# Two-layer graph network on one core: the first two basis products of the first layer as 15 block products of thirds

## The chip, the core and the metric

The kernel runs on one core of a Trainium2 chip. TensorE (PE) multiplies and writes its results to PSUM, which has eight banks; VectorE (DVE) and ScalarE (ACT) read PSUM and do elementwise work; GpSimd (POOL) and SyncE (SP) issue most DMAs here. Each engine has its own queue and works through it in order; semaphores hold an instruction until what it needs is there. The metric is the device time in microseconds. All values are fp32.

## The reference, cut to what matters

A block of graph attention over 384 nodes comes first, then a relational graph convolution of two layers (the node feature width is 768, with six relations and four bases):

```python
def _rgcn_conv(x, src, dst, edge_type, basis, comp, root, bias):
    W = jnp.einsum('rb,bio->rio', comp, basis)
    h_all = jnp.einsum('ni,rio->rno', x, W)
    ...
    agg = jax.ops.segment_sum(msg, dst, num_segments=n)
    return agg + x @ root + bias
...
x = jax.nn.relu(h_text @ w_in + b_in)
for l in range(L):
    h_in = x
    x = _rgcn_conv(x, src, dst, edge_type, basis[l], comp[l], root[l], conv_bias[l])
    x = jax.nn.relu(x)
    x = x + h_in
    x = _batchnorm(x, bn_gamma[l], bn_beta[l])
```

The kernel computes the sum in another order: for each basis b it forms H_b = x · basis[l, b], a product of a 384x768 by a 768x768 matrix, and then multiplies the four H_b by four 384x384 matrices At_b, which are the normalised counts of edges A_r weighted with comp (the "mixes").

## The kernel before, in words

**Stages.** Layer norm and attention take the first part of the run. The projection `w_in` then leaves its result transposed in `XT`: 128 partitions, six chunks of 128 features, 384 nodes. Each of the two layers then has four bases, the product with `root`, the product with At and the batch norm. PE, DVE, ACT, POOL and SP run in program order (`manual_schedule`), so the order of the Python code is the order in each queue.

**One base.** For a base the weights lie in three tiles `w[0]` to `w[2]`, each 128 partitions by 2 by 768. Of the three blocks of 128 nodes, the third (n = 2) is multiplied directly (banks `pe` and `pf`, 12 products of 384 columns). Nodes 0 and 1 go by a product of 2x2 blocks that needs seven block multiplications in place of eight: `pa`, `pb`, `pc`, with the node sums `S` (from `node_sums`, L915, once a layer) and the weight sums `T` and `T4` (from `weight_sums`, L923, and `last_sums`, L932, for each base; nine VectorE operations). That is 21 products of 384 columns, so 33 in a base. `rest()`, the last block of a base, is issued inside the next base. The results go to `H_` by copies on ACT and additions on DVE (L991 to L1002).

**Banks.** `next_bank` takes the PSUM bank that was used longest ago among those allowed; `ring` holds the order.

**Loads.** `wload` puts a tile of 768 KB into one of five buffers (`wpool`), as four DMAs on SP. `w_first`, five of these tiles, is issued during attention; `load_basis` issues the rest.

**Work put between.** `go_between(l, b, c)` issues, at fixed places in bases 2 and 3 of the first layer, what prepares At: `share(r)` (L358: a matmul with ones, two ACT operations, a reciprocal and a multiplication on DVE) and `mix` (L341: At from A; 20 of these operations of VectorE follow the last addition of base 3). The counts A come from tables in memory, gathered by POOL's DMAs at L850 to L854 after its last scatter.

**Room.** `S`, `T4` and `H_` live in a pool `cp` that is opened when the attention pool closes; `T` takes the buffers tagged `hT` and `mask8`. In the stage after the bases, `spaces` (L1025 to L1035) reuses such room for the feature sums.

Of the kernel before, what the change touches and what calls it, by code (L numbers as in the profile page):

```python
# [10 lines left out]
F32 = mybir.dt.float32  # L11
# [3 lines left out]
AF = mybir.ActivationFunctionType  # L15
# [12 lines left out]
KC = DC // P  # L28
HC = DC // 2
HN = N // 2  # L30
R = 6
# [12 lines left out]


BQ, BK, BV, BIQ, BIK, BIV, B_IN, CB, GAM, BET, NCOL = 0, 8, 16, 24, 32, 40, 48, 54, 66, 78, 90

# [4 lines left out]
def gnn_kernel(ctx: ExitStack, tc: tile.TileContext, out, x, edges, chunks, cols, rows, small,  # L52
               wq, wk, wv, wiq, wik, wiv, wo, w_in, basis, root, w_out):
    nc = tc.nc
# [298 lines left out]
    def add_up(r):  # L353
        sums[r] = late.tile([P, N], F32, tag="sum", name="sum", bufs=4)
        nc.gpsimd.tensor_tensor(sums[r], A[:, r, 0, :], A[:, r, 1, :], ALU.add)
        nc.gpsimd.tensor_tensor(sums[r], sums[r], A[:, r, 2, :], ALU.add)

    def share(r):  # L358

        ps = next_bank("ps_cnt", [i for i in range(8) if i not in taken])  # L360
        nc.tensor.matmul(ps[:, :N], ones, sums[r], start=True, stop=True)
        rn = late.tile([P, N], F32, tag="rn", name="rn", bufs=2)

        nc.scalar.activation(rn, ps[:, :N], AF.Relu, bias=minus)
        nc.scalar.activation(rn, rn, AF.Identity, bias=ones[:, 0:1])
        nc.vector.reciprocal(rn, rn)
        nc.vector.tensor_tensor(A[:, r], A[:, r], rn[:, None, :].to_broadcast([P, NT, N]), ALU.mult)
        if r + 4 < R:
            add_up(r + 4)


    with ExitStack() as inner:
# [262 lines left out]
        At = late.tile([P, B, NT, N], F32, name="At")  # L635
        A = late.tile([P, R, NT, N], F32, tag="A", name="A")

        prA = keep.tile([P, KD, N], F32, tag="hT", name="prA")
# [92 lines left out]
        for g in range(STEPS + 1):  # L731
            f = g + LEAD
            if g < STEPS:
                turn_probs(g)
            if f < STEPS:
                exponents(f)
            if f - 1 in total:
                normalise(f - 1)
            if f + 1 < STEPS:
                scores(f + 1)  # L740
            if g == STEPS:
                ps_y = next_bank("ps_y", (0,))
                multiply_o(ps_y, 2, 0, range(KD - 1))
            if g > 0:
                gather(g - 1)
            if f + 2 == STEPS:

                w_x = [act_tile("w_x") for _ in range(2)]
                for half in range(2):
                    load_rows(w_x[half], w_in[half])  # L750
                w_first = [wload(basis[0, 0, part], (2, DC), "w_c") for part in range(3)]
                w_first += [wload(basis[0, 1, part], (2, DC), "w_c") for part in range(2)]
        soft_stack.close()
# [152 lines left out]
    with tc.tile_pool(name="conv", bufs=1) as cp:  # L906
# [4 lines left out]
        def block(X, n, i):  # L911

            return X.rearrange("p (c i) n -> p i c n", i=2)[:, i, :, n * P:(n + 1) * P]

        def node_sums(X):  # L915
            S = cp.tile([P, 4, 3, P], F32, tag="S", name="S")
            for i, a, b, op in ((0, block(X, 1, 0), block(X, 1, 1), ALU.add), (1, S[:, 0], block(X, 0, 0), ALU.subtract),
                                (2, block(X, 0, 0), block(X, 1, 0), ALU.subtract),
                                (3, block(X, 0, 1), S[:, 1], ALU.subtract)):
                nc.vector.tensor_tensor(S[:, i], a, b, op)  # L920
            return S

        def weight_sums(w):  # L923
            T13 = keep.tile([P, 3, 2, HC], F32, tag="hT", name="T13")
            T2 = keep.tile([P, 3, HC], F32, tag="mask8", name="T2")
            for c in range(3):
                nc.vector.tensor_tensor(T13[:, c], w[c][:, :, HC:], w[c][:, 0, :].rearrange("p (o d) -> p o d", o=2),
                                        ALU.subtract)
                nc.vector.tensor_tensor(T2[:, c], w[c][:, 1, HC:], T13[:, c, 0], ALU.subtract)
            return T13[:, :, 0], T2, T13[:, :, 1]  # L930

        def last_sums(w, T2):  # L932
            T4 = cp.tile([P, 3, HC], F32, tag="T4", name="T4")
            for c in range(3):
                nc.vector.tensor_tensor(T4[:, c], w[c][:, 1, :HC], T2[:, c], ALU.subtract)
            return T4

        w_first = [w_first[:3], w_first[3:]]

        def load_basis(l, b):  # L940
            w = w_first.pop(0) if w_first else []
            return w + [wload(basis[l, b, part], (2, DC), "w_c") for part in range(len(w), 3)]

# [17 lines left out]

        S = node_sums(XT)
        w = load_basis(0, 0)
        T = weight_sums(w)
        for l in range(L):

            H_ = cp.tile([P, B, NT, DC], F32, tag="H", name="H")
            rest = lambda: None
            for b in range(B):
                hs = [[H_[:, b, n, i * HC:(i + 1) * HC] for i in range(2)] for n in range(NT)]  # L970
# [21 lines left out]
                nc.vector.tensor_tensor(hs[0][0], hs[0][0], pb, ALU.add)  # L992
                times(pc, S[:, 0], lambda c: T[0][:, c], True)
                nc.scalar.copy(hs[2][0], pe)
                nc.scalar.copy(hs[2][1], pf)
                nc.scalar.copy(hs[1][1], pc)
                times(pa, S[:, 1], lambda c: T[1][:, c])
                nc.scalar.copy(hs[0][1], pa)
                times(pc, S[:, 3], lambda c: w[c][:, 1, HC:])
                nc.vector.tensor_tensor(hs[0][1], hs[0][1], pc, ALU.add)  # L1000
                times(pa, S[:, 2], lambda c: T[2][:, c])
                nc.vector.tensor_tensor(hs[1][1], hs[1][1], pa, ALU.add)  # L1002
# [14 lines left out]
            for k in range(KC):  # L1017
# [5 lines left out]
                go_between(l, B, k)  # L1023
            room2 = keep.tile([P, KD * N], F32, tag="hT", name="room2")
            spaces = [room2[:, 2304:]]  # L1025
            if l + 1 < L:
                spaces += [v.rearrange("p i k o -> p (i k o)")[:, i * 768:(i + 1) * 768] for v, n in
                           ((cp.tile([P, 4, 3, P], F32, tag="S", name="sums"), 2),
                            (wpool.tile([P, 2, 6, P], F32, tag="w", name="sums"), 2)) for i in range(n)]
                spaces.append(cp.tile([P, 3, HC], F32, tag="T4", name="sums").rearrange("p c d -> p (c d)")[:, :768])  # L1030
                w = load_basis(l + 1, 0)
# [48 lines left out]
            T1, T2 = [room2[:, i * 1152:(i + 1) * 1152].rearrange("p (c d) -> p c d", c=6) for i in range(2)]  # L1080
            T4 = keep.tile([P, 6, HN], F32, tag="mask8", name="T4")
            nc.vector.tensor_tensor(T1, q(0, 1), q(0, 0), ALU.subtract)
# [187 lines left out]
```

## Time and profile before

| what | value |
|---|---|
| runs | 725.38 us median of 3 (724.61 to 729.79) |
| profiled execution: its own time | 717.47 us |
| profiled execution: span | 715.7 us, 9149 instructions |
| TensorE clock granted | 0.995 |
| PE busy | 699.9 us (98%) |
| DVE busy | 512.6 us (72%) |
| first layer's base 0 starts | 370.89 us |
| first layer's four bases end, but for the last rest() | 458.9 us |

The span runs from the first to the last instruction that the profiler shows; the execution's own time is 1.8 us longer. Matmuls are pipelined: a listed duration of one matmul includes its way through the array, so the pace is read from the starts of a row of them. An fp32 product of one 128x128 block is two passes, so two rows of the trace. In a timeline or chain the columns are the start in us, the length in us, and what ran.

### The profile page before, as it was taken

To read this page: it belongs to the slowest core of one execution; us is meant where nothing else is said; L and a number is where in the kernel's file an instruction comes from. 1 tells how busy PE (TensorE), PEld (TensorE's weight loads), DVE (VectorE), ACT (ScalarE), POOL (GpSimd) and SP (SyncE) were. 2 spreads that over 40 slices of the span, in tenths; PEclk is the share of its full clock that TensorE was granted. 3 is DMA by queue.
4 is the path that set the end of the run, shared out by engine and by line. 5 is a ranking of instruction groups with operands and counts; after the bars stand their busy time and mean duration, and the time that the engine had idled before them with its cause. 6 is when DMAs were issued, how large, how long until landed. Compare 5 with 4: busy or idle time off the path is not lost.

```text
span 715.7 us, 9149 instructions
## 1 busy us (share of the span) xinstructions
PE 699.9 (98%) x3228; PEld 527.9 (74%) x3228; DVE 512.6 (72%) x1307; ACT 157.6 (22%) x360; POOL 308.1 (43%) x239
## 2 busy tenths in 40 slices
PE   8999999999999999999999999999999999999995
PEld 7759999999997444478985555558975555579943
DVE  5886697868886699787534279798878766507756
ACT  3211111111111577410221124202131111011100
POOL 1366777778687788687786542000000000120000
PEclk9999999999999999999999999999999999999999
DMA  8788787373562622733424994311104322700001
GB/s 303 267 279 264 228 250 212 80 243 67 203 209 43 177 2 1 221 44 45 89 0 103 250 288 153 133 44 45 45 0 133 102 69 94 308 1 1 1 30 59
DMA packets 69180, 91.04 MB, mean 127 GB/s; under 512 B 22940, under 2 KB 50688, under 8 KB 68750
## 3 DMA queue, kind: packets, MB, share of 16 engines
q1 hardware_dynamic: 46830, 78.45, 32.6%
q0 software_dynamic: 21296, 9.60, 10.8%
q10 hardware_dynamic: 1008, 2.41, 0.9%
q8 instruction: 25, 0.41, 0.2%
q14 instruction: 21, 0.17, 0.1%
HBM read 79.27 MB, written 11.16 MB: 126 GB/s over the span
## 4 chain that ended last, share of the span: by engine, by line
PE 87%; DVE 10%; ACT 2%; DMA 1%; issue 0%; DVEq 0%; ACTq 0%
PE ps_g L985 12%; PE ps_g L979 10%; PE ps_k L402 10%; PE ps_c L1077 10%; PE ps_v L402 8%; PE ps_q L420 6%; PE ps_q L402 5%; PE ps_f L1183 4%; DVE At L348 4%; PE ps_y L402 3%; PE ps_c L1019 3%; PE ps_x L402 3%; PE ps_o L707 2%; PE ps_s L662 2%; PE ps_pT L696 2%; PE ps_v L586 2%
## 5 line engine op out<-in xcount | busy, mean ns | idle before, releaser
L283 POOL DMA_INDIRECT atab<-count,at x99 | 166.3, 1679 | 44.2 <-issue 23.5
L278 POOL DMA_INDIRECT mtab<-m_val,at x99 | 103.4, 1045 | 57.6 <-issue 22.9
L1170 POOL TENSOR_TENSOR x_sb<-x_sb,room 128x1024 f32<-128x1024 f32 x3 | 7.0, 2348 | 188.9 <-DMA room<-in_rows 188.9
L348 DVE SCALAR_TENSOR_TENSOR At<-A,small_sb,At 128x1152 f32<-128x1152 f32 x40 | 53.6, 1414 | 0.0
L979 PE MATMUL ps_g<-T,S 128*128 128x384 f32 x144 | 49.1, 486 | 0.0
L985 PE MATMUL ps_g<-w_c,XN 128*128 128x384 f32 x144 | 47.7, 487 | 1.1 <-DVE XN L1107 1.1
L985 PE MATMUL ps_g<-w_c,XT 128*128 128x384 f32 x144 | 47.9, 486 | 0.0
L420 PE MATMUL ps_q<-hT,w_q 128*128 128x384 f32 (+1 forms) x160 | 43.4, 435 | 1.4 <-DVE hT L108 1.4
L985 PEld LDWEIGHTS ps_g<-w_c,XN 128*128 128x128 f32 x144 | 27.3, 190 | 20.2 <-DVE XN L1107 1.4
L979 PEld LDWEIGHTS ps_g<-T,S 128*128 128x128 f32 x144 | 27.3, 190 | 19.2 <-ACT H L991 0.4
L985 PEld LDWEIGHTS ps_g<-w_c,XT 128*128 128x128 f32 x144 | 27.3, 190 | 18.8
L420 PEld LDWEIGHTS ps_q<-hT,w_q 128*128 128x128 f32 x160 | 30.1, 200 | 14.1 <-ACT hT L101 1.7
L1077 PE MATMUL ps_c<-At,H 128*128 128x192 f32 x216 | 36.4, 326 | 0.0
L1077 PEld LDWEIGHTS ps_c<-At,H 128*128 128x128 f32 x216 | 35.4, 190 | 0.5
L402 PE MATMUL ps_k<-T,S 128*128 128x192 f32 x192 | 35.1, 326 | 0.0
L1107 DVE TENSOR_TENSOR XN<-XN,ps_c 128x192 f32<-128x192 f32 x38 | 12.5, 349 | 30.8 <-ACT XN L1063 19.7
L402 PEld LDWEIGHTS ps_k<-T,S 128*128 128x128 f32 x192 | 31.8, 190 | 0.0
L1183 PE MATMUL ps_f<-w_out,XN 128*128 128x512 f32 (+1 forms) x84 | 31.1, 531 | 0.0
L675 DVE CUSTOM_DVE_ANT_0 s<-ps_s,mask 128x384 f32<-128x384 f32 x48 | 24.5, 550 | 5.3 <-PE ps_s L662 5.3
L267 DVE SCALAR_TENSOR_TENSOR same<-cells,own,later 128x128 f32<-128x128 int32 x99 | 28.0, 350 | 0.4
L267 DVE SCALAR_TENSOR_TENSOR same<-keys,key,weigh 128x128 f32<-128x128 int32 x99 | 27.9, 349 | 0.0
L1183 PEld LDWEIGHTS ps_f<-w_out,XN 128*128 128x128 f32 x84 | 15.9, 190 | 14.9 <-issue 14.3
(298 smaller groups left out, 1411.6 us busy)
## 6 DMA issues: line engine op xcount, KB each, us to landing
w_c<-in_basis SPq DMA_DIRECT2D x96, 192.0 KB, 4.1
atab<-zero SPq DMA_DIRECT2D x36, 192.0 KB, 5.2
A<-atab POOLq DMA_DIRECT2D x12, 576.0 KB, 9.0
keys<-keys_d SPq DMA_DIRECT2D x25, 192.0 KB, 5.1
w_c<-in_root SPq DMA_DIRECT2D x6, 768.0 KB, 7.1
w_q<-in_wiq SPq DMA_DIRECT2D x16, 256.0 KB, 6.4
w_k<-in_wk SPq DMA_DIRECT2D x16, 256.0 KB, 5.8
w_k<-in_wik SPq DMA_DIRECT2D x16, 256.0 KB, 3.0
```

The costliest lines, as they stand in the source:

```text
L267: nc.vector.scalar_tensor_tensor(same, row[:, n, :], mine[:, c:c + 1], times, ALU.is_equal, ALU.mult, accum_out=count[:, i, c:c + 1])
L278: nc.gpsimd.indirect_dma_start(mtab[c // PER][:, :], bass.IndirectOffsetOnAxis(at[:, 0, c:c + 1], 0), m_val[:, c:c + 1], None)
L283: nc.gpsimd.indirect_dma_start(atab[0 if i < 11 else i % 2][:, :], bass.IndirectOffsetOnAxis(at[:, 1, c:c + 1], 0), count[:, 1, c:c + 1], ...
L348: nc.vector.scalar_tensor_tensor(At[:, b], A[:, r], w, At[:, b], ALU.mult, ALU.add)
L402: nc.tensor.matmul(ps, a[:, k, :], b[:, k, :], start=start and k == 0, stop=(k == 3), skip_group_check=not start)
L420: nc.tensor.matmul(ps[o][:, c], wt_[:, k, o * P:(o + 1) * P], src[:, k, c], start=(k == 0 and c.start == 0), stop=(k == KD - 1 and c.stop ...
L675: nc.vector.tensor_tensor_reduce(s[j], ps[:, :N], mask8[:, t, :], -scale, 3.0e38, ALU.add, ALU.min, tops[:, j:j + 1])
L979: nc.tensor.matmul(ps, x[:, c], y(c), start=start and c == 0, stop=(c == 2), skip_group_check=not start)
L985: nc.tensor.matmul(ps, block(XT, n, i)[:, c], w[c][:, i, o * HC:(o + 1) * HC], start=(first and c == 0), stop=(c == 2 and (i == 1 or ps is ...
L1019: nc.tensor.matmul(pr[o], w[k // 2][:, k % 2, o * P:(o + 1) * P], XT[:, k, :], start=(k == 0), stop=(k == KC - 1))
L1077: nc.tensor.matmul(ps, x[:, c], y[:, c], start=start and c == 0, stop=stop and c == 5, skip_group_check=True)
L1183: nc.tensor.matmul(p, XT[:, k, t * P:(t + 1) * P], w[k // 2][:, k % 2, c0:c1], start=(k == 0), stop=(k == KC - 1))
```

## The change

For the first layer's bases 0 and 1 the product is formed in another way. The output has three blocks of nodes and three blocks of 256 features (`HC2`, "thirds"); the inner dimension has two blocks of 384. A product of [3,2] blocks by [2,3] blocks has 18 block products; the tables `X_SUMS`, `W_SUMS` and `PRODUCTS` write it with 15, from sums and differences of blocks. The 11 sums of nodes are formed once, for base 0, and used again for base 1; the 10 sums of weights are formed for each base. A product is three matmuls of 256 columns. Four PSUM accumulators a base (`c` in `PRODUCTS`) are added up over several products, and are read in between: each reading goes to one or more blocks of `H_`, as ACT's copy where the block is written first and as DVE's addition or subtraction afterwards. Bases 2 and 3, and all of the second layer, keep the old form; for layer 0 their `node_sums` and first `weight_sums` are issued after the new bases. The weights of bases 0 and 1 are laid out by thirds in memory (`thirds`), and loaded by thirds; the sixth of these tiles and the three of base 2 are issued between the products. The sums lie in `x_all`, `w_room`, `mroom` and `room2`, which also serve as `S`, `T`, `T2`, `T4` and `spaces` afterwards. The changed lines of `add_up` and `share` only put the six small tiles into one (`sum_room`).

```diff
+X_SUMS = (          # (to, sign, a, sign, b)
+    (6, 1, 2, -1, 4),
+    (7, -1, 5, -1, 6),
+    (8, 1, 1, 1, 3),
+    (9, 1, 6, -1, 8),
...
+    (16, -1, 1, -1, 5),
+)
+W_SUMS = (          # (to, sign, a, sign, b, step at which it is issued)
+    (6, 1, 2, 1, 5, -2),
+    (7, 1, 1, 1, 6, -1),
+    (8, 1, 4, 1, 7, 0),
+    (9, 1, 0, -1, 6, 1),
+    (10, 1, 1, 1, 2, 2),
+    (11, 1, 3, 1, 9, 4),
+    (12, 1, 4, 1, 11, 5),
+    (13, 1, 0, -1, 2, 6),
+    (14, 1, 12, -1, 13, 9),
+    (15, -1, 1, -1, 12, 10),
+)
+PRODUCTS = (        # (x, w, accumulator, ((to, sign), ...))
+    (2, 1, 0, ((4, 1),)),
+    (6, 6, 1, ((7, 1), (8, -1))),
+    (7, 7, 0, ((7, 1),)),
+    (5, 8, 2, ((7, 1),)),
+    (9, 9, 1, ((6, -1),)),
+    (10, 10, 0, ((8, -1),)),
+    (3, 4, 3, ((4, 1),)),
+    (11, 5, 0, ((5, -1),)),
+    (12, 12, 3, ((3, -1),)),
+    (13, 13, 0, ((2, 1),)),
+    (8, 11, 3, ((0, 1), (6, -1))),
+    (14, 0, 1, ((0, 1), (2, 1))),
+    (15, 14, 0, ((0, 1), (3, -1))),
+    (0, 15, 3, ((1, -1),)),
+    (16, 3, 0, ((6, -1),)),
+)
...
-                w_first = [wload(basis[0, 0, part], (2, DC), "w_c") for part in range(3)]
-                w_first += [wload(basis[0, 1, part], (2, DC), "w_c") for part in range(2)]
+                def load_third(b, t):
+                    parts[b, t] = wload(thirds[b, t], (KC, HC2), "w_c")
+
+                for b, t in ((0, 2), (0, 1), (0, 0), (1, 2), (1, 1)):
+                    load_third(b, t)
...
+        x_all = cp.tile([P, 4 * 3 * N], F32, name="x_all")
+        x_room = [x_all[:, i * 3 * N:(i + 1) * 3 * N] for i in range(4)]
+        room2 = keep.tile([P, KD * N], F32, tag="hT", name="room2")
+        mroom = keep.tile([P, 6, HN], F32, tag="mask8", name="mroom")
...
+        w_room = cp.tile([P, 3, HC2], F32, name="w_room")
+        x_sums = [v[:, i * N:(i + 1) * N].rearrange("p (c n) -> p c n", c=3) for v in x_room for i in range(3)]
+        w_places = [w_room, mroom.rearrange("p c n -> p (c n)")[:, :DC].rearrange("p (c o) -> p c o", c=3)]
+        w_places += [room2[:, i * DC:(i + 1) * DC].rearrange("p (c o) -> p c o", c=3) for i in range(4)]
...
+        def signed_sum(dst, sa, a, sb, b):
+
+            if sa > 0:
+                nc.vector.tensor_tensor(dst, a, b, ALU.add if sb > 0 else ALU.subtract)
+            elif sb > 0:
+                nc.vector.tensor_tensor(dst, b, a, ALU.subtract)
+            else:
+                nc.vector.scalar_tensor_tensor(dst, a, -1.0, b, ALU.mult, ALU.subtract)
+
+        def x_block(i):
+            return XT[:, i % 2 * 3:i % 2 * 3 + 3, i // 2 * P:(i // 2 + 1) * P] if i < 6 else x_sums[i - 6]
+
+        def w_block(g, i):
+            return parts[g, i % 3][:, i // 3 * 3:i // 3 * 3 + 3, :] if i < 6 else w_sums[g, i]
...
+        def bases_by_15():
...
+            todo = sorted(todo + [(first[x[0]] - 3, 2, 0, i) for i, x in enumerate(X_SUMS)])
+            chain, begun = {}, set()
+            for step in range(NPROD * BY_15):
+                g, k = step // NPROD, step % NPROD
+                while todo and todo[0][0] <= step:
+                    _, kind, *what = todo.pop(0)
+                    if kind == 1:
+                        sum_weights(*what)
+                    else:
+                        _, sa, a, sb, b = X_SUMS[what[1]]
+                        signed_sum(x_sums[what[1]], sa, x_block(a), sb, x_block(b))
+                x, w, c, targets = PRODUCTS[k]
+                start = (g, c) not in chain
+                if start:
+                    bank_ = next_bank("ps_g", free_banks())
+                    held.append(ring[-1])
+                    chain[g, c] = bank_[:, :HC2], ring[-1]
+                ps, index = chain[g, c]
+                x, w = x_block(x), w_block(g, w)
+                for j in range(3):
+                    nc.tensor.matmul(ps, x[:, j], w[:, j], start=start and j == 0, stop=(j == 2),
+                                     skip_group_check=not start)
+                for to, sign in targets:
+                    n, t = to // 3, to % 3
+                    dst = H_[:, g, n, t * HC2:(t + 1) * HC2]
+                    if (g, to) in begun:
+                        nc.vector.tensor_tensor(dst, dst, ps, ALU.add if sign > 0 else ALU.subtract)
+                    elif sign > 0:
+                        nc.scalar.copy(dst, ps)
+                    else:
+                        nc.scalar.activation(dst, ps, AF.Identity, scale=-1.0)
+                    begun.add((g, to))
+                if not any(p[2] == c for p in PRODUCTS[k + 1:]):
+                    held.remove(index)
+                if (g, k) == (0, 7):
+                    load_third(1, 0)
+                elif (g, k) in ((0, 10), (0, 14), (1, 8)):
+                    basis_loads.append(wload(basis[0, len(basis_loads)], (2, DC), "w_c"))
...
-        S = node_sums(XT)
-        w = load_basis(0, 0)
-        T = weight_sums(w)
         for l in range(L):
 
             H_ = cp.tile([P, B, NT, DC], F32, tag="H", name="H")
             rest = lambda: None
-            for b in range(B):
+            if l == 0:
+                bases_by_15()
+                w = load_basis(0, BY_15)
+                T = weight_sums(w)
+                S = node_sums(XT)
+            for b in range(0 if l else BY_15, B):
...
-                spaces += [v.rearrange("p i k o -> p (i k o)")[:, i * 768:(i + 1) * 768] for v, n in
-                           ((cp.tile([P, 4, 3, P], F32, tag="S", name="sums"), 2),
-                            (wpool.tile([P, 2, 6, P], F32, tag="w", name="sums"), 2)) for i in range(n)]
-                spaces.append(cp.tile([P, 3, HC], F32, tag="T4", name="sums").rearrange("p c d -> p (c d)")[:, :768])
+                spaces += [x_all[:, i * 768:(i + 1) * 768] for i in range(5)]
```

The comments behind the three table names are not in the code; they name the columns. Operands 0 to 5 are blocks of `XT` or of the weights themselves, 6 and up are sums, which the other texts call X6, W6 and so on; products are counted from 0.

## The prediction

> **What bounds the kernel now.** I read the page's busy table first, then the chain that ended last in order of time, then the timelines of TensorE and VectorE around the first layer's bases.
>
> ```profile
> PE 699.9 (98%) x3228; PEld 527.9 (74%) x3228; DVE 512.6 (72%) x1307; ACT 157.6 (22%) x360; POOL 308.1 (43%) x239
> 370.89 11.61 PE ps_g L985 x36
> 382.50 7.74 PE ps_g L979 x24
> 390.24 3.87 PE ps_g L985 x12
> 394.11 1.94 PE ps_g L979 x6
> 459.46 26.58 DVE At L348 x20
> ```
>
> The reader is to see that in the bases the chain is nothing but matmuls, piece touching piece, with no other engine between; further on, at 459.46, it passes to VectorE's mixes. So a microsecond of TensorE work taken from the first two bases moves the end by a microsecond, provided VectorE starts those mixes earlier too (they follow base 3's last sum, so they do).
>
> One base of the old form is 33 products of 384 columns; each fp32 product is two passes in the trace, so 66 passes. 12 passes take 3.87 us, which is 322.5 ns each, and the base 11.61 + 7.74 + 1.94 = 21.29 us (the 3.87 in between is the next base's start). Bases 0 and 1 are thus 42.57 us, 370.89 to about 413.5, without a TensorE wait between them.
>
> **Matmuls.** The new form has 15 products of 3 blocks: 45 matmuls of 256 columns, 90 passes a base. A row of the same width is in the trace:
>
> ```profile
> 332.45 3.45 PE ps_y L840 x16
> L1077 PE MATMUL ps_c<-At,H 128*128 128x192 f32 x216 | 36.4, 326 | 0.0
> L1077 PEld LDWEIGHTS ps_c<-At,H 128*128 128x128 f32 x216 | 35.4, 190 | 0.5
> ```
>
> 16 passes of 256 columns in 3.45 us are 215.6 ns each. 90 × 215.6 = 19.40 us a base, 38.80 for two: **3.77 us less**, if nothing is waited for. (A product is then 6 passes, 1.293 us.)
>
> A rule speaks against this: the change has 180 weight loads where there were 132. The Trainium skill ("TensorE: Matmul & The Clock Gate", Part 3, The mechanism) says that a weight load overlaps matmuls in flight only when it targets other row groups, and all of these fill the array. By the rule the 48 extra loads cost 48 × 190 ns = 9.1 us, and the change loses 5.3. The two rows of L1077 are the measurement: loads of 190 ns and matmuls listed at 326 ns fill the same stretch, the loads with hardly an idle ns, and 8 such passes start every 1.30 us (162.5 ns each, in the chain at L402). A full-array load is hidden there. At 256 columns there are 215.6 ns to hide 190 in. I take the row.
>
> **VectorE.** The old two bases gave it 4 node sums, 18 weight sums and 6 additions, 18.0 us busy of 42.6. The new ones give it 20 weight sums of 128x768, 11 node sums of 128x384, 20 additions from PSUM of 128x256:
>
> ```profile
> 373.38 0.95 DVE L927 TENSOR_TENSOR T<-w_c 128x768 f32<-128x768 f32 x1
> 374.37 0.56 DVE L929 TENSOR_TENSOR T<-w_c,T 128x384 f32<-128x384 f32 x1
> 374.85 0.95 DVE L927 TENSOR_TENSOR T<-w_c 128x768 f32<-128x768 f32 x1
> 310.20 0.42 DVE L803 TENSOR_TENSOR x_sb<-ps_y,x_sb 128x256 f32<-128x256 f32 x1
> ```
>
> By duration 19.0 + 6.1 + 8.4 = 33.5 us. The rows overlap a little: L929 lasts 0.56 and the next starts 0.48 after it. I use start to start: 0.88 for a weight sum, 0.47 for a node sum, 0.36 for an addition, 0.1 more where the next reads the last one's result. Base 0 then needs 8.8 + 5.2 + 3.6 = 17.6 of its 19.4 us, base 1, which reuses the node sums, 12.4. The average fits; the start doesn't, because 8 of the weight sums and 8 of the node sums are queued by product 6.
>
> So I go through base 0 in program order (VectorE takes sums of step k, then additions of product k, then sums of step k+1), times from TensorE's start at 370.87. An addition can begin 0.20 after its product's last pass and TensorE goes on 0.06 after what it waits for; both are read at the 0.45 us wait of 369.32, where an addition of 368.91 to 369.26 releases TensorE. First the start: the first sum goes into w_room, new memory where the attention pool was, and the second weight sum into mroom, whose tag holds the T4 that the last input product reads until 370.89 + 0.17. VectorE itself is idle from 369.26. The trace can't show whether w_room and x_all wait for the same product. If not, two sums are early; I take that they wait, since w_x[1], which that product reads, held that stretch as far as I can lay the pools out.
>
> With the first sum at 0.18: W6 0.18, X6 1.06, W7 1.53, X7 2.41, W8 2.88, then step 1's W9 3.76, X8 4.64, X9 5.21, step 2's W10 5.68, X10 6.56. Product 1 needs X6 (TensorE waits 0.37), product 2 needs X7 (0.06), product 4 needs X9 (0.21). The additions of products 2 and 3 come only at 7.03 and 7.39, behind those sums, and product 5 writes the bank that product 2's addition reads: 0.41. Then W11, X11, W12, X12 push the addition of product 5 to 10.45, which product 7's bank waits for: 0.83; that of product 6 holds product 8: 0.42. From product 9 on VectorE is ahead and stays so; in base 1 nothing waits. Sum **2.30 us lost**. With w_room free at once it is 0.95.
>
> A second rule would make this worse. The skill ("VectorE: DVE Perf Modes", The DRAIN you can't avoid) has the next operation wait until the pipe has emptied; that page itself lets one that isn't held start earlier. By full durations (0.96, 0.57, 0.43) the same walk loses 3.9 us. The trace starts L927 0.48 after L929, so I use 2.3 and keep 3.9 for the range.
>
> **The seam to base 2.** Base 1's accumulators take the ring's last four banks, so pa of base 2, its first matmul, is the bank of base 1's product 14, whose result VectorE adds last. TensorE waits 0.20 + 0.42 + 0.06 = **0.68 us**; the old seam had none, since base 1's rest() was done inside base 2. Between 0 and 0.7; the 0.45 wait at 369.32 is the nearest row, and I take 0.68.
>
> **What else moves.** Node sums (2.00 us) now stand behind base 2's weight sums (4.39): with T4 (1.40) and three shares (421.61 to 433.35, 11.74) VectorE has 19.5 us of work, ready about 20.1 after base 2 begins. The node sums themselves come 6.9 after it and TensorE wants them after 36 passes and 3 counts, 13.6. Before, VectorE was through 22.0 after base 2's start (411.36), with TensorE at 23.2; now TensorE is at 21.3, having no rest(). The cover is 1.2 us in both: nothing is paid. Without it each microsecond would be TensorE's.
>
> Loads: SP now issues four weight tiles (16 DMAs of 192 KB) behind products 7, 10 and 14 of base 0 and 8 of base 1. The third (1,0) goes out near 383, before the gathers of A saturate DMA (they begin at 386.43), and is wanted by W9 of base 1 near 394. The last part of base 2 goes out near 404 and is wanted near 415; in the saturated stretch the trace took 409.67 to 418.74, 9.1 us, for such a part. Both are covered by about 2 us or more; a sum that waited there would hold every addition behind it, hence TensorE. POOL's sums for shares are ready 9 us or more before their use (416.96 against 426.19 for the third). The later use of x_all for `spaces`, in place of S, T4 and a weight tile, adds no instruction. ScalarE has 19 or so reads of some 0.4 us: its idle time covers them.
>
> **Sum.** 3.77 − 2.30 − 0.68 = 0.8 us gained. Against the profiled execution (717.47, span 715.7) that is 716.7; the median of the runs shown is 7.9 us above that execution, so 725.38 − 0.8 = **724.6 us**. About 1%, 7 us, is what a measurement of this kernel can tell from no change; the three runs alone span 5.2.
>
> **Rivals.**
> - *The gain nearly whole (0.2).* w_room is free at once, the sums run ahead: 3.77 − 0.95 = 2.8 less a seam of 0 to 0.68: 722.6 to 723.2. For it: VectorE's 1.6 us of idle time before the base. Against it: W7 must wait anyway.
> - *VectorE becomes the bound of base 0 (0.25).* One mechanism: more sums ahead of the additions than TensorE's 1.29 us a product cover, and an accumulator bank held by a late addition. At full durations 3.9 are lost, 3.77 − 3.9 − 0.68 = −0.8: 726.2; if mixed strides or POOL's traffic slow each operation by another 10%, near 728. It decides from 3.1 us lost, reached at about 0.92 a weight sum and 0.52 a node sum. Against it: 0.88 and 0.47 in the rows.
> - *A load is late (0.05).* Part (1,0) lands after 394 and base 1 starves; each microsecond counts whole, 726 to 735.
> - *Not the work it says (0.02):* weight loads unhidden, 5 us slower, 730; the rows exclude it nearly.
>
> The forecast, a gain of 0 to 2 us, has 0.48. Range: from 3.1 gained with a point of run scatter, 720.5, to slow sums with the same, 729.5. Over 1% faster would need more than the whole 3.77, so only scatter gives it: 0.04. Over 1% slower needs a late load or something unseen: 0.09. Within 1%: 0.87.
>
> **What would show it.** Right: 180 passes of 128x256 into ps_g, starting every 215 ns; TensorE's waits for VectorE all in the first nine products, about 2.3 us, and one of some 0.7 at base 2's first matmul; VectorE near 33 us busy in the two bases; base 2 beginning some 41.8 after the first product. Wrong: waits in base 1, VectorE waiting for a DMA of thirds, weight loads apart from matmuls, or base 2 waiting for S.

## The result, and the profile after

The change makes no difference that can be measured. Over 20 runs each the changed kernel has a median of 728.50 us (721.60 to 743.94) and the kernel before 727.65 (723.45 to 734.86); the ratio is 0.9999, with a 95% interval of 0.9976 to 1.0021. The ratio leaves out slow executions, more than 1.5% above the fastest of the same kernel: four of the changed kernel and one of the kernel before. Timed again, 13 runs against 17, it was 716.25 against 716.02 us, ratio 1.0003 (0.9990 to 1.0015). The absolute times differ by some 12 us from one comparison to the other for both kernels, so only ratios from one comparison are used, and beside them stretches of the trace.

The page of the changed kernel, in the rows that were shown for the kernel before:

```profile
span 724.3 us, 9303 instructions
PE 698.2 (96%) x3276; PEld 534.0 (74%) x3276; DVE 532.1 (73%) x1334; ACT 158.4 (22%) x366; POOL 314.6 (43%) x239
```

The span is 8.6 us longer than the 715.7 of before, with TensorE less busy. That is not the change: base 0 began at 370.72 before and begins at 378.64 here, 7.9 us later, after code in which the change touches only the weights that are loaded and where tiles lie (in two other profiles it was the other way round, 372.65 before and 369.27 changed), and from the first mix to the end of the span it is 256.3 and 256.1 us. What the change does lies between. I read two stretches: **A**, from base 0's first pass to base 2's first pass, and **B**, from there to the first mix of VectorE. For the kernel before, A is its two bases of 42.57 us, and B the other 46.09 of its 88.66. The first mixes, which end B, before and in the changed kernel:

```profile
459.38 2.74 DVE L348 SCALAR_TENSOR_TENSOR At<-A,small_sb,At 128x1152 f32<-128x1152 f32 x2
```

```profile
468.20 2.74 DVE L398 SCALAR_TENSOR_TENSOR At<-A,small_sb,At 128x1152 f32<-128x1152 f32 x2
```

The timeline of TensorE in stretch A of the changed kernel (start, length in us, engine, line, result and operands, count of passes; in brackets the idle time before it and its releaser):

```profile
378.64 1.46 PE L1072 MATMUL ps_g<-w_c,XT 128*128 128x256 f32 x6
380.42 1.53 PE L1072 MATMUL ps_g<-w_room,x_all 128*128 128x256 f32 x6 [0.32 <-DVE x_all L1019]
...
387.53 1.46 PE L1072 MATMUL ps_g<-w_c,XT 128*128 128x256 f32 x6
389.79 1.56 PE L1072 MATMUL ps_g<-w_c,x_all 128*128 128x256 f32 x6 [0.80 <-DVE H L1078]
...
394.15 1.46 PE L1072 MATMUL ps_g<-room,x_all 128*128 128x256 f32 x6
395.44 1.46 PE L1072 MATMUL ps_g<-w_c,x_all 128*128 128x256 f32 x6
...
418.75 1.46 PE L1072 MATMUL ps_g<-w_c,x_all 128*128 128x256 f32 x6
420.73 4.14 PE L1134 MATMUL ps_g<-w_c,XT 128*128 128x384 f32 x12 [0.52 <-DVE H L1078]
```

From 394.15 to 395.44 and on to base 2 a product starts every 1.29 to 1.30 us, the forecast pace. Against that pace products 1 to 9 are 2.58 us late in sum, and base 2's first pass 0.69 (420.73, where 418.75 + 1.29 = 420.04). A is 42.09 us, 0.48 less than the old 42.57. B is 47.47, 1.38 more than 46.09. The place where B loses it, TensorE in base 2:

```profile
434.38 2.10 PE L1128 MATMUL ps_g<-room,x_all 128*128 128x384 f32 x6
437.50 2.20 PE L1128 MATMUL ps_g<-mroom,x_all 128*128 128x384 f32 x6 [1.03 <-ACT H L1140]
```

The second product should start 1.94 us after the first and starts 3.12 after it, so 1.18 are lost (the 1.03 in brackets is the listed idle time alone): pa can't be written until ScalarE has copied it (L1140). ScalarE's own timeline says why it is late, and VectorE's what it is waiting for:

```profile
435.86 0.58 ACT L414 ACTIVATE sum_room<-ps_cnt,minus 128x384 f32<-128x384 f32 x1 [4.57 <-DVE A L417]
436.47 0.62 ACT L415 ACTIVATE sum_room<-sum_room,ones 128x384 f32<-128x384 f32 x1
436.99 0.46 ACT L1140 COPY H<-ps_g 128x384 f32<-128x384 f32 x1
```

```profile
421.57 1.24 DVE L991 TENSOR_TENSOR mroom<-w_c,room 128x384 f32<-128x384 f32 x1
422.73 1.75 DVE L989 TENSOR_TENSOR room<-w_c 128x768 f32<-128x768 f32 x1
...
428.79 1.35 DVE L982 TENSOR_TENSOR x_all<-XT,x_all 128x384 f32<-128x384 f32 x1
...
434.10 1.67 DVE L417 TENSOR_TENSOR A<-A,sum_room 128x1152 f32<-128x1152 f32 x1
```

ScalarE's operation for share(2) stands in its queue ahead of the copy. It writes the slot of `rn` (two slots, r % 2) that VectorE's multiplication for share(0), L417, still reads. That multiplication ends at 435.77, 15.0 us after base 2's start, because VectorE has the weight sums, the node sums and T4 in front of it, and because some rows last up to 0.8 us longer than the 0.95 and 0.56 that the same shapes have elsewhere. In the same time POOL adds up the counts:

```profile
420.69 1.70 POOL L405 TENSOR_TENSOR sum_room<-A 128x384 f32<-128x384 f32 x1 [3.48 <-DMA A<-atab]
422.47 1.19 POOL L406 TENSOR_TENSOR sum_room<-sum_room,A 128x384 f32<-128x384 f32 x1
```

Its rows are longer too (0.98 is their shortest). Those shown of the two engines lie over each other.

### The profile page after: what moved, and what is told of

It reads as the page before. It is cut to its first block, busy times and chain, and to the rows that moved or that the text cites. A ratio compares the mean times of both kernels' runs of the same rounds, so it can differ in the third digit from the quotient of the medians.

```text
span 724.3 us, 9303 instructions
## 1 busy us (share of the span) xinstructions
PE 698.2 (96%) x3276; PEld 534.0 (74%) x3276; DVE 532.1 (73%) x1334; ACT 158.4 (22%) x366; POOL 314.6 (43%) x239
## 5 line engine op out<-in xcount | busy, mean ns | idle before, releaser
L328 POOL DMA_INDIRECT mtab<-m_val,at x99 | 108.4, 1095 | 53.0 <-issue 27.4
L470 PE MATMUL ps_q<-hT,w_q 128*128 128x384 f32 (+1 forms) x160 | 41.8, 422 | 1.4 <-DVE hT L158 1.4
L470 PEld LDWEIGHTS ps_q<-hT,w_q 128*128 128x128 f32 x160 | 28.5, 190 | 14.1 <-ACT hT L151 1.7
L1128 PE MATMUL ps_g<-room,x_all 128*128 128x384 f32 x72 | 25.2, 486 | 0.0
L1134 PE MATMUL ps_g<-w_c,XT 128*128 128x384 f32 x72 | 24.3, 487 | 0.5 <-DVE H L1078 0.5
L1168 PE MATMUL ps_c<-XN,w_c 128*128 128x384 f32 x72 | 23.5, 486 | 0.0
L1168 PE MATMUL ps_c<-XT,w_c 128*128 128x384 f32 x72 | 23.5, 486 | 0.0
```

The costliest lines, as they stand in the source:

```text
L328: nc.gpsimd.indirect_dma_start(mtab[c // PER][:, :], bass.IndirectOffsetOnAxis(at[:, 0, c:c + 1], 0), m_val[:, c:c + 1], None)
L470: nc.tensor.matmul(ps[o][:, c], wt_[:, k, o * P:(o + 1) * P], src[:, k, c], start=(k == 0 and c.start == 0), stop=(k == KD - 1 and c.stop ...
L1128: nc.tensor.matmul(ps, x[:, c], y(c), start=start and c == 0, stop=(c == 2), skip_group_check=not start)
L1134: nc.tensor.matmul(ps, block(XT, n, i)[:, c], w[c][:, i, o * HC:(o + 1) * HC], start=(first and c == 0), stop=(c == 2 and (i == 1 or ps is ...
L1168: nc.tensor.matmul(pr[o], w[k // 2][:, k % 2, o * P:(o + 1) * P], XT[:, k, :], start=(k == 0), stop=(k == KC - 1))
```

## The experiments

My theory after the profile: stretch A gains what the queues of base 0 and the seam leave of the 3.77 us, and stretch B gives it back, since VectorE's cover in base 2 is gone. For B there were two sub-theories: POOL and VectorE holding each other up (theory 1), and the moved node sums alone (theory 2). The rival for the whole: the readings of accumulators, not VectorE's sums, cost A its time, or the gain is lost behind the mixes.

What all profiles show, in us; "gather" is the time from base 0's first pass to POOL's first load of A. The waits are the listed idle times; that of the first sums early is too short to be listed and is taken from start to start:

| kernel | gather | A | B | wait in B before pa or a count | first pass to first mix |
|---|---|---|---|---|---|
| before | 15.7 | 42.57 | 46.09 | none | 88.66 |
| before, again | 21.5 | 42.57 | 46.10 | none | 88.67 |
| changed | 12.6 | 42.09 | 47.47 | 1.03 | 89.56 |
| changed, again | 12.8 | 42.08 | 47.17 | 0.72 | 89.25 |
| changed, timed again | 21.5 | 42.14 | 47.91 | 1.47 | 90.05 |
| without POOL's additions | 5.1 | 42.08 | 46.14 | none | 88.22 |
| node sums behind product 10 | 7.3 | 43.24 | 46.20 | none | 89.44 |
| node sums behind product 8 | 22.1 | 42.07 | 46.28 | none | 88.35 |
| three rn slots | 18.7 | 42.14 | 46.20 | none | 88.34 |
| without the sums | 14.1 | 39.52 | 46.20 | none | 85.72 |
| first sums early | 20.8 | 40.71 | 46.56 | 0.28 | 87.27 |
| seam alone | 21.4 | 41.46 | 49.05 | 2.70 | 90.51 |
| three repairs | 17.0 | 40.03 | 46.09 | none | 86.12 |
| five repairs | 20.8 | 39.13 | 47.60 | 1.24 | 86.73 |

Every kernel also has the wait of some 0.6 us for ScalarE's copy at the end of base 2's rest(), which the kernel before has as well.

**The changed kernel again.**

> The changed kernel once more, for a second profile. Two stretches are read: A, from the first pass of base 0 to the first pass of base 2 (42.1 us in the first profile), and B, from there to the first mix on VectorE (47.5 us; 46.1 in the kernel before, its rest() of 1.9 us left out). If A follows from the two queues alone it is 42.1 again within 0.2. If B's loss of 1.4 us comes from where POOL's sums for the shares fall against VectorE's sums, B can differ, by up to 1.5 us, when POOL's last scatter stands otherwise against base 0 (12.6 us after its start in the first profile); if it comes from the moved node sums alone, B is 47.5 again and VectorE's rows L989 and L991 keep their stretched durations (1.75, 1.24 us) only by chance.

A came out at 42.08: it repeats to 0.01 us. B was 47.17 with a wait of 0.72, so it moves from profile to profile while A doesn't. The stretched rows were there again, over other instructions:

```profile
443.53 1.23 DVE L991 TENSOR_TENSOR mroom<-w_c,room 128x384 f32<-128x384 f32 x1
444.69 1.75 DVE L989 TENSOR_TENSOR room<-w_c 128x768 f32<-128x768 f32 x1
```

POOL's additions stood at 442.79 to 445.62 this time, over these two rows.

**Without POOL's additions.**

```diff
-        sums[r] = sum_room[:, r % 4]
-        nc.gpsimd.tensor_tensor(sums[r], A[:, r, 0, :], A[:, r, 1, :], ALU.add)
-        nc.gpsimd.tensor_tensor(sums[r], sums[r], A[:, r, 2, :], ALU.add)
+        sums[r] = A[:, r, 0, :]
```

> Leaves out POOL's two additions for each share (the count of each share is taken from one of its three node blocks alone), so that POOL does no arithmetic in base 2. Theory 1 (VectorE and POOL hold each other up when both work on SBUF with two inputs): VectorE's weight and node sums in base 2 all last their 0.95 and 0.56 us, the queue reaches share(0)'s multiplication 3.4 us earlier, ScalarE doesn't wait for it, TensorE's 1.03 us wait for the copy of pa is gone, B is near 46.1 to 46.3. Theory 2 (the moved node sums alone used up the cover): durations in base 2 stay stretched or don't matter, and the wait stays at 0.5 to 1 us, B 47.

B fell to 46.14 and the wait went. The groups of VectorE's weight and node sums in base 2 (line, operation, shapes and count; busy us, mean ns) have their plain durations:

```profile
L987 DVE TENSOR_TENSOR room<-w_c 128x768 f32<-128x768 f32 x3 | 2.9, 952 | 0.0
L989 DVE TENSOR_TENSOR mroom<-w_c,room 128x384 f32<-128x384 f32 x3 | 1.7, 558 | 0.1
```

In the changed kernel the same two groups, there L989 and L991, are the following:

```profile
L989 DVE TENSOR_TENSOR room<-w_c 128x768 f32<-128x768 f32 x3 | 3.6, 1216 | 0.0
L991 DVE TENSOR_TENSOR mroom<-w_c,room 128x384 f32<-128x384 f32 x3 | 2.4, 784 | 0.1
```

So the stretching comes from POOL's additions. The Trainium skill has the rule ("GPSIMD Engine Reference", 1. Specifications): POOL shares its SBUF interfaces with VectorE and contends with VectorE instructions that take two inputs from SBUF. The trace agrees, and gives the price, about 0.8 us for a VectorE row that meets one of POOL's additions; VectorE's reciprocals, which have one input, keep 2.54 us.

The same trace gives the cover that base 2 has with plain durations. These are share(0)'s multiplication and the first operation of share(2), which waits only for its count:

```profile
459.70 1.36 DVE L415 TENSOR_TENSOR A<-A,sum_room 128x1152 f32<-128x1152 f32 x1
463.26 0.58 ACT L412 ACTIVATE sum_room<-ps_cnt,minus 128x384 f32<-128x384 f32 x1 [3.29 <-PE ps_cnt L409]
```

The first ends 11.65 us after base 2's start (449.41) and the second begins 13.85 after it: 2.20 us of cover, with the node sums in VectorE's queue. In the three unchanged profiles the multiplication ends 3.39, 3.08 and 3.82 us later than that, so it should cost TensorE 1.19, 0.88 and 1.62 us; from start to start TensorE lost 1.18, 0.88 and 1.62.

**The node sums behind product 10, and behind product 8.**

```diff
+                if (g, k) == (1, 10):
+                    first_S.append(node_sums(XT))
...
                 T = weight_sums(w)
-                S = node_sums(XT)
+                S = first_S.pop()
```

The second version has (1, 8) in place of (1, 10). The four results lie in slots of `x_all` that base 1 has read by then.

> The four node sums of bases 2 and 3 are issued behind product 10 of base 1, where VectorE was idle for 3.4 us, and lie in slots that base 1 no longer reads; nothing else changes. Theory 2 (moved node sums): VectorE reaches share(0) 2.0 us earlier and TensorE's wait for the copy of pa (1.03 us) goes, B 46.1 to 46.3, A 42.1. Theory 1 (contention with POOL): the weight sums stay stretched by about 1.5 us, the node sums aren't touched by POOL in their new place, so the wait goes too or shrinks below 0.3, but some rows of 128x768 still last over 1.2 us.

B fell to 46.20, as theory 2 had it, but A rose to 43.24. VectorE's 3.4 us of idle time end before product 10's addition, not after it, since the queue stands at that addition; behind it, the node sums held up the next additions and so the accumulators: there are two more waits, at 32.8 and 41.2 us of A. Here the gather stood at 7.3 us, far ahead, so this run alone doesn't settle B.

> The node sums of bases 2 and 3 now behind product 8 of base 1, ahead of W14, so that they fill VectorE's 3.4 us of idle time and no addition stands behind them that TensorE wants (behind product 10 they had cost A 1.16 us). A 42.1, B 46.1 to 46.3, no wait for the copy of pa in base 2, though rows of weight sums stretched by POOL remain. If B keeps a wait over 0.5 us, the node sums were not what used up the cover.

In the idle time proper, A is 42.07, B 46.28, without a wait, and with the gather at 22.1, a place near that of the slowest unchanged profile. So taking away either the contention or the 2 us of node sums is enough. Theory 2 alone fails, since it wanted the wait to stay without POOL's additions, and so does contention alone: the stretched rows were still here (1.75 and 1.23 us for two of the weight sums). With the node sums in place the cover is 2.2 us, and the wait is what the stretching exceeds it by.

**Three rn slots.**

```diff
-        rn = sum_room[:, 4 + r % 2]
+        rn = sum_room[:, 4 + r % 3]
```

> Three slots in place of two for the reciprocal counts of share, so that ScalarE's work for share(2) doesn't wait for VectorE's multiplication of share(0). VectorE's order and POOL's additions stay. If the wait in base 2 is handed on by ScalarE's queue (share(2), then the copy of pa), the 1.0 us wait of TensorE goes and B is 46.1 to 46.4 with the stretched rows still there. If TensorE lacks VectorE's own results (S or T), the wait stays, with VectorE as its releaser.

B was 46.20, with no wait for the copy. But this profile doesn't test the slot, because VectorE wasn't late in it: its rows were stretched by only 1.5 us, and share(0)'s multiplication ended at 426.11, before share(2)'s count was there, so two slots would have done as well:

```profile
424.75 1.36 DVE L417 TENSOR_TENSOR A<-A,sum_room 128x1152 f32<-128x1152 f32 x1
426.84 0.58 ACT L414 ACTIVATE sum_room<-ps_cnt,minus 128x384 f32<-128x384 f32 x1 [3.29 <-PE ps_cnt L411]
```

That ScalarE's queue, share(2) ahead of the copy, hands VectorE's lateness on is read from the traces in which it was late: the three unchanged ones, the first sums early and the seam alone. In all five share(2) begins 0.09 to 0.10 us after share(0)'s multiplication ends, and the copy stands behind it. That a third slot takes the wait away is not shown.

**Without the sums.** All 31 sums of the two bases are left out, and products take plain blocks.

> Leaves out the 31 sums of nodes and weights of the two new bases (products take plain blocks in their place); products, readings and loads stay. If VectorE's queue of sums costs the 2.3 us that were forecast (2.1 measured by the waits of the first nine products), A falls from 42.1 to 39.2 or 39.4: 38.8 of matmuls and the seam of 0.5. If the waits come from the accumulators being read in between, whatever VectorE has ahead, A stays above 40.5.

A fell from 42.08 to 39.52: 38.80 of matmuls and 0.69 of seam make 39.49. In the trace the passes at the start stand in one piece:

```profile
394.55 9.66 PE L1067 MATMUL ps_g<-w_c,XT 128*128 128x256 f32 x44
```

The readings of accumulators alone cost nothing; VectorE's sums ahead of them cost 2.56 us. B was 46.20 without a wait, though base 2 had its node sums and POOL's additions here: they stretched VectorE's rows by 1.9 us, which is within the cover of 2.2.

**The first sums early.**

```diff
-        w_places = [w_room, mroom.rearrange("p c n -> p (c n)")[:, :DC].rearrange("p (c o) -> p c o", c=3)]
-        w_places += [room2[:, i * DC:(i + 1) * DC].rearrange("p (c o) -> p c o", c=3) for i in range(4)]
+        w_places = [room2[:, i * DC:(i + 1) * DC].rearrange("p (c o) -> p c o", c=3) for i in range(4)]
+        w_places += [w_room, mroom.rearrange("p c n -> p (c n)")[:, :DC].rearrange("p (c o) -> p c o", c=3)]
...
+            todo[1], todo[2] = todo[2], todo[1]
```

> The weight sums take room2's four slots first (free since the last product that reads h2T) and w_room and mroom afterwards, and W7 is issued ahead of X6; nothing else changes. If the start of base 0 is late because the first sum's room is read by the last product of the input projection (VectorE idle 1.66 us before it), W6 starts some 1.6 us earlier against base 0's first pass, W7 too, and the waits of the first nine products fall from 2.6 us to 0.2 to 0.8: A 40.0 to 40.4 (42.08 before). If the backlog of 16 sums by product 6 sets the waits wherever the first ones start, A falls by less than 0.6. B as in the unchanged kernel, 47.2 to 47.5.

In the changed kernel VectorE sat idle for 1.66 us until TensorE's last product of the input projection let go of the room (first row below); with room2's slots first, W6 and W7 start before that product is through (second and third; base 0 starts at 369.22):

```profile
378.84 0.96 DVE L1019 TENSOR_TENSOR w_room<-w_c 128x768 f32<-128x768 f32 x1 [1.66 <-PE ps_x L452]
```

```profile
367.68 0.95 DVE L1019 TENSOR_TENSOR room<-w_c 128x768 f32<-128x768 f32 x1
368.67 0.96 DVE L1019 TENSOR_TENSOR room<-w_c,room 128x768 f32<-128x768 f32 x1
```

A fell by 1.37, to 40.71, a little less than the 1.7 to 2.1 expected, because the wait before product 7 stayed with 0.54: the addition of product 5 is queued behind W12 and X12. B, at 46.56, was better than expected; its place against POOL had moved.

**The three repairs together**: room2 first, node sums behind product 8, and base 1's accumulator 0 kept out of base 2's banks (`taken[:] = [chain[1, 0][1]]` after the loop over steps).

> All that the profiles point to together: the first weight sums in room2 ahead of X6, the node sums behind product 8 of base 1, and base 1's accumulator 0 kept out of base 2's five banks, so that pa doesn't wait for the last addition. A 39.3 to 39.8 (38.8 of matmuls), B 46.1 to 46.3, from base 0's first pass to the first mix 85.5 to 86.1 us against 88.7 in the kernel before: 2.6 to 3.2 us less, a ratio of 0.9957 to 0.9965, if nothing else in the run moves. If the saving were lost behind the mixes, the ratio would be 1 with these stretches.

The stretch from first pass to first mix is 86.12 us, 2.54 less than before, with A 40.03 and B 46.09; A is a quarter of a microsecond above what was expected, by the same wait before product 7. The time was 714.88 us against 716.00, ratio 0.9984 (0.9971 to 0.9996), so less than half of the 2.6 to 3.2 us expected. The profiled run, 713.25, is the fastest of 14 (up to 717.73); the others must have lost something that it didn't, and what it was isn't shown.

**The unchanged change, timed again.**

> The changed kernel timed again, beside the one that follows. Its three profiles so far give 88.3 to 89.6 us from base 0's first pass to the first mix (those with two rn slots 89.3 and 89.6), the kernel before 88.7. If the run's time follows this stretch, the ratio is 0.999 to 1.002. If the changed kernel has a cost or gain elsewhere, the ratio stands off from 1 by more than 0.002.

The ratio was 1.0003 (0.9990 to 1.0015). The profile shows 90.05 us, and the largest wait of the unchanged order, 1.47.

**Five repairs**: the three above, three rn slots, and node sums two products ahead of their use in place of three.

> As the version that joined the three repairs, and further: node sums are issued two products ahead of their use in place of three, so that fewer of them stand in front of the additions that free accumulator banks, and share has three rn slots. If the last wait of base 0 (0.54 us before product 7, for product 5's addition) comes from sums queued ahead of additions, it goes and A falls from 40.03 to 39.2 to 39.6; first pass to first mix 85.3 to 85.9; ratio to before 0.996 to 0.998. If it comes from the accumulators alone, A stays at 40.0.

A fell to 39.13, so the last wait of base 0 did come from sums queued ahead of additions: no wait of TensorE is listed in A any more. But in B a new wait appeared, on a count that POOL hadn't ready:

```profile
422.74 0.91 PE L411 MATMUL ps_cnt<-sum_room,ones 128*128 128x384 f32 x2 [1.24 <-POOL sum_room L406]
```

POOL's chain (scatters, then loads of A, then additions) doesn't come forward with TensorE. So the stretch was 86.73, longer than expected. The time was 714.15 us against 716.02, ratio 0.9966 (0.9947 to 0.9985), from 6 runs against 17; the 1.9 us less are those of the stretch. All six (712.02 to 714.90) lie below every run of the kernel before (from 715.81) and of the changed kernel (from 715.47) timed beside them, so this version is faster than both, by a third of a per cent. Whether it is faster than the three repairs isn't shown: the intervals overlap.

**The seam alone.**

> Only the seam: base 1's accumulator 0 is kept out of base 2's five banks. If TensorE waits at base 2's first pass for VectorE's last addition out of that bank, the wait of 0.51 goes and A falls from 42.08 by 0.6 to 0.7 to 41.4; base 2's VectorE work, then 0.6 later against TensorE, may give up to that much back as a longer wait for the copy of pa in base 2. If something else holds base 2's first pass, A stays 42.08.

A was 41.46, 0.61 to 0.68 less than in the unchanged profiles, as the wait for the bank went. B rose to 49.05: the wait for the copy of pa was 2.70. A TensorE that is earlier waits longer for the same VectorE, and in this profile POOL's additions lay badly too; the seam's gain was more than lost.

**The kernel before, again.**

> The kernel before once more, for a second profile of the stretch from base 0's first pass to the first mix (88.66 us in the first, with POOL's gather of A beginning 15.7 us after base 0; in the changed kernel 88.3 to 90.1, the longest with the gather beginning 21.5 us after it). If the loss in base 2 belongs to the changed kernel's order, this stretch is 88.7 again whatever the gather's place, without a wait for the copy of pa in base 2. If it belongs to POOL's place alone, the stretch is over 89.5 when the gather begins some 21 us after base 0.

The stretch was 88.67, to 0.01 us that of the first profile, and without a wait for the copy, although POOL's additions met VectorE's weight sums here as well:

```profile
413.96 2.22 DVE L927 TENSOR_TENSOR T<-w_c 128x768 f32<-128x768 f32 x1
416.22 1.23 DVE L929 TENSOR_TENSOR T<-w_c,T 128x384 f32<-128x384 f32 x1
```

In the old order share(0)'s multiplication ended at 425.70 all the same, 3.27 us before share(2) began (in the first profile 1.43 before it, after a wait of 3.70 for a weight tile):

```profile
424.34 1.36 DVE L367 TENSOR_TENSOR A<-A,rn 128x1152 f32<-128x1152 f32 x1
428.97 0.58 ACT L364 ACTIVATE rn<-ps_cnt,minus 128x384 f32<-128x384 f32 x1 [3.29 <-PE ps_cnt L361]
```

The old order bears the contention, the new one bears 2.2 us of it. The old one has no node sums here, and its base 2 holds base 1's rest(), so ScalarE's share(2) comes 1.8 us later against the start of base 2.

## Why the prediction was right, point by point

*The number.* 724.6 us was forecast, in a range of 720.5 to 729.5, and 728.50 measured. That this lies inside is in part luck: the range is 9 us wide, and the 724.6 rests on 725.38 for the kernel before, the median of three runs, where that of 20 is 727.65. The gain of 0.8 us did not come. Base 2 began 42.09 us after the first product, where some 41.8 were said, so 0.5 of the 0.8 were there in A; base 2 took them back.

*The bound.* Right as long as base 2 doesn't wait: with the three repairs both A and the stretch are 2.54 us shorter than before. With the seam alone A fell by 0.6 to 0.7 and the stretch grew by 0.5 to 1.3. The time after the mixes stayed, 256.3 and 256.1 us. The two stretches account for the null result: −0.4 to −0.5 in A, +1.1 to +1.8 in B. In sum the three profiles of the changed kernel are 0.6 to 1.4 us longer in them, where a gain of 0.8 was forecast; timed beside each other the kernels differ by +0.2 us (−0.7 to +1.1).

*Matmuls.* Right: 1.29 to 1.30 us a product. The weight loads stay hidden; these are the rows of one group. (The section that the prediction cites against it also has a load into the background weight buffer pulled ahead of matmuls in flight, so the page as a whole doesn't say that these loads would be exposed.)

```profile
L1072 PE MATMUL ps_g<-room,x_all 128*128 128x256 f32 x54 | 13.1, 382 | 0.0
L1072 PEld LDWEIGHTS ps_g<-room,x_all 128*128 128x128 f32 x54 | 10.1, 190 | 2.1 <-DVE x_all L1021 0.4 <-issue 0.3
```

*The start of base 0.* Right in mechanism, place and nearly in size. W6 started 0.20 us after base 0's first pass (0.18 said, counted from 370.87, where the timeline has the first pass at 370.72); the late products were the ones named. The sum was 2.58 in place of 2.30: where TensorE stops, the restart takes about 0.1 us more than the walk gave it, seen as rows of 1.53 and 1.56 in place of 1.46. Start-to-start durations were the right choice over full ones, as 42.08 repeated to 0.06 us in all unchanged A stretches; full ones would have made it 43.4.

*The seam.* 0.68 said, 0.69 measured, and gone when the bank was another.

*VectorE's busy time in A.* 33 said, 30.74 measured in the stretch.

*Loads.* No wait of VectorE for a third or a weight tile in A, as said.

*Base 2.* This is the step that failed: "The cover is 1.2 us in both: nothing is paid." It cost 0.7 to 1.5 us of waiting in the three unchanged profiles, 1.1 to 1.8 in B. I had looked for TensorE's need of VectorE's own results (S, T, the additions), and those did come in time. Two terms were missing: that ScalarE's copy of pa stands behind share(2), which needs VectorE to have finished share(0), and POOL's additions, which make VectorE's rows longer there. The first brings a date forward: VectorE must be through with share(0) by the 14th microsecond of base 2, where I had only asked it to be through with everything by the end. At that date the cover is 2.2 us, not 1.2, with plain durations; the rows stretched by POOL's additions then took 3.1 to 3.8. "Base 2 waiting for S" was named as a sign of being wrong; base 2 did wait, but for pa's copy. The trace of before had a hint: the prediction says that in the bases the chain that ended last is nothing but matmuls, yet at the start of base 3 it runs through ScalarE from 435.44 to 441.73. There too a copy that TensorE needs (L1006, at 441.25) stands behind ScalarE's work for At, mostly this:

```profile
436.67 4.58 ACT At L346 x4
```

*POOL's sums.* "Ready 9 us or more before their use" did not hold in general: the third was ready 10.1, 8.6 and 1.9 us before its use in the three unchanged profiles (at 423.66, used at 433.73, in the first), the last with a later gather, and with the five repairs, 3 us faster with a late gather, it was 1.24 late.

*The rivals.* The nearly whole gain didn't come: w_room did wait. VectorE as the bound of base 0 was half true, by 2.6 of the 3.1 us from which it was to decide. What brought the change to nothing was outside all rivals, a wait in base 2.

## What to carry to other kernels

A block product with fewer multiplications pays only what its sums leave: here 3.8 us of matmuls were saved, and a burst of sums at the start, a bank at the seam and a lost cover in the next base took it all back. When work is moved in front of a queue of another engine, look for the earliest instruction of any third engine that waits on that queue (a slot used again, a copy standing behind it), not for the last consumer. Ordering the sums so that results that free a PSUM bank don't stand behind them, and putting the first ones into room that is free early, kept part of the gain: 0.34% with a 95% interval of 0.15 to 0.53%.

## What the runs showed of the hardware that I had not expected

When one of POOL's two-input additions (128x384) meets a two-input operation of VectorE in SBUF, VectorE's row lasts longer: 0.95 us became 1.75 and, with the seam alone, 2.27, and 0.56 became 1.24 and, with the five repairs, 2.58. Without POOL's additions they were 952 and 558 ns again. POOL's own rows, 0.98 at the shortest, lasted up to 2.22 there, but no run shows that VectorE is the cause: in the changed kernel one of 1.53 (412.59) stands where VectorE is idle. The place of these meetings differs from run to run, since POOL's gather begins 5 to 22 us after base 0's start, so a stretch with little cover differs too (B from 47.17 to 47.91), while one with cover repeats to some hundredths.

In several profiles of the shared code before base 0 TensorE also waited for reasons that the trace doesn't name, up to 7.2 us at a time in the k projection; base 0 then began at up to 407 us where the quickest began at 369. What causes these waits stays open. They are not the change's: the kernel before, run beside four of these profiles, took 743.68 us, where it took 716 beside others.
